# A wait for an earlier landing at every fourth gather of a graph layer's edge messages

## The chip, the cores and the metric

The kernel runs on one core of one Trainium2 chip. The metric is the device time of one execution in microseconds (us). A core has engines that run side by side, each with its own list of instructions: PE multiplies matrices, DVE and ACT do vector and scalar work, POOL issues the gathers here, and SP issues the other transfers. They meet at semaphores: an instruction may wait until a count has been reached, and everything behind it on its engine waits with it.

## The reference

There are 12500 nodes with 256 features and 212500 edges, sorted by their target node. Each edge has a source, a target and one of 8 types.

```python
h = jnp.maximum(_layernorm(x, axis=-1), 0.0)
hx = einsum('ni,rio->rno', h, weight)          # one 256 x 256 matrix for each type
agg = segment_sum(hx[edge_type, src], dst)     # sum over the edges of each target
out = x + 0.5**0.5 * agg + h_bias + 0.5**0.5 * (h @ loop_weight)
```

## The kernel before

**Sums before products.** The matrix of a type is the same for all its edges, so the kernel sums the rows of `h` first, by target and type, and multiplies afterwards. The edges are cut into 1583 tiles of 128, numbered `t`; two tiles make a unit (`PAIR` = 2). For each tile POOL gathers the 128 source rows (128 x 256 numbers, 131 KB) from DRAM into a tile `msg` (`gather`, line 832). The first 100 tiles read `x` and are normalised on the chip; the 1483 others read the table `h` that the kernel has written by then.

**The sums.** PE multiplies the gathered rows by a matrix of zeros and ones, `oh`, which DVE has made from targets and types (`edge_sums`, line 885; four matmuls for a tile, into the PSUM tile `ps`). DVE adds `ps` to a ring of sums `acc` (line 909). When all edges of a group of 128 nodes are in, PE multiplies that part of the ring by the weights (line 1070, 32 matmuls and 4 for the nodes' own rows), DVE adds the bias and `x` (lines 1083 and 1084), and SP stores four groups at a time, with loads of the next `x` and `h` rows (lines 1020 and 1089).

**Order.** Everything stands in the order in which the program issues it (a manual schedule). One loop runs over the tiles; for each `t` it issues the gathers up to `goal(t)`, then the sums of tile `t`, then bits of the other work by their costs and due times. `goal(t)` is `t + 65` (`AHEAD` = 64), less at the start.

**The gathers' own limits.** `msg` has 66 places, given out two at a time, so the gather of an even tile waits until PE has read the unit that had this place, 66 tiles earlier. It also waits on its own landing counter (eight of them, in turn), which the gather eight tiles in front of it used. Up to tile 103 a gather also waits for the last matmul of the newest unit issued so far: those gathers go "no faster than the sums". From tile 104 on nothing else holds a gather back. POOL has hardly any other work.

Of the kernel before, what the change touches and what calls it, by code (L numbers as in the profile page):

```python
# [17 lines left out]
SYNC_DEP = mybir.DependencyInfo(mybir.DependencyClass.Sync, mybir.DependencyReason.DATA)  # L18
# [36 lines left out]
QUAD = 4  # L55
LEAD = 4
PAIR = 2
# [167 lines left out]
def kernel(  # L225
# [56 lines left out]
    def place_of(t):  # L282
        u, i = divmod(t, PAIR)
        half = 0 if PAIR * u + 1 == NT else PAIR - 1 - i
        return u // P, half, u % P


    with ExitStack() as main:
# [531 lines left out]
        def gather(t):  # L820
            if t % PAIR == 0:
                both = msgs.tile([P, PAIR, D], F32, name="msg")
                for i in range(PAIR):
                    msg[t + i] = both[:, i, :]
            if t % QUAD:
                kind[t] = kind[t - 1]
            else:
                kind[t] = "h" if state["h32"] is not None and t >= state["h32"] + LATE else "x"
            table = {"h": h32, "x": x}[kind[t]]
            b, i, u = place_of(t)  # L830
            at = i * P + u
            i = nc.gpsimd.indirect_dma_start(  # L832
                out=msg[t], out_offset=None, in_=table[:, :],
                in_offset=bass.IndirectOffsetOnAxis(ap=gidx[b][:, at : at + 1], axis=0))
            if t < STARTED + STEEP * (AHEAD - STARTED) and "unit" in latest:
                tc.add_manual_dep(
                    i.ins, latest["unit"], SYNC_DEP, reason="no faster than the sums")

        def goal(t):

            return min(t + AHEAD + 1, STARTED + STEEP * (t // PAIR * PAIR))
# [50 lines left out]
            return ps  # L892

        sums = {}
        latest, made = {"pe": None}, {}

        order = RING + WIN

# [217 lines left out]
        with tc.manual_schedule():  # L1116
# [19 lines left out]
            for t in range(min(STARTED, NT)):  # L1136
                gather(t)
# [94 lines left out]
            for t in range(NT):  # L1232
                done["tile"] = t
                while gathered < min(NT, goal(t)):
                    gather(gathered)
                    gathered += 1
# [121 lines left out]
```

## Time and profile before

| | |
|---|---|
| Median of 3 runs | 2395.17 us (2394.54 to 2396.05) |
| The profiled execution: its time, its span | 2423.11 us, 2421.4 us |
| PE busy with matmuls | 1958.0 us, 81% of the span |
| DVE, POOL busy | 1328.4 us (55%), 1507.4 us (62%) |
| Granted PE clock, mean | 0.901 |
| Gathers (line 832) | 1583, from 4.9 us to 2335.6 us |
| Gathers' packets | 207.59 MB, 29.5% of 16 DMA engines' span |

How to read the profile: PE is TensorE's matmuls, PEld its weight loads, and each instruction has the line of the source that made it. A row `out<-in` tells what is written from what. In brackets behind an instruction stands how long its engine had been idle before it, and what ended the idle time; "issue" means that the engine waited for nothing that the profile shows, "remote" that the releaser could not be named. A gather on POOL is shown for as long as POOL writes its descriptors, not until its data are there; when they land is read from the packets and semaphore records of the same trace.

### The profile page before, as it was taken

Reading aid. Unit: us, or ns where it says so; the run is one execution under the profiler, and the core shown is the slowest. Engines: PE = TensorE matmul, PEld = TensorE weight load, DVE = VectorE, ACT = ScalarE, POOL = GpSimd, SP = SyncE. Lnnn points to the kernel's source line nnn. Section 1 sums busy time; section 2 is a strip of 40 time slices with the busy share of each in tenths; the row PEclk is TensorE's granted clock in tenths of the full one; section 3 lists DMA queues with packets and bytes.
Section 4 is the critical chain, followed back from the end, with each engine's and each line's share of the span. In section 5 each row is a group of like instructions: output and inputs, shape, how many; then the busy total and the mean of one; then the engine's idle time right before and its main releaser. Section 6 shows DMA issues by size and latency. Waiting matters only on the chain. (4 is left out here: it accounts for less than half of the span.)

```text
span 2421.4 us, 28275 instructions
## 1 busy us (share of the span) xinstructions
PE 1958.0 (81%) x10171; PEld 1693.8 (70%) x10171; DVE 1328.4 (55%) x3162; ACT 186.6 (8%) x363; POOL 1507.4 (62%) x1608
## 2 busy tenths in 40 slices
PE   2357888888888888888888888788888888888899
PEld 1256677777677777777777777777777777777788
DVE  5668344445655446654446654555755545655453
ACT  6653000000000000000000000000000000000000
POOL 6566666666666666666666666666666666666630
PEclk9578989898999998999988989999899899988999
DMA  7973433433333333333343333343343333343320
GB/s 235 306 227 86 125 92 114 123 91 116 115 90 116 104 112 114 92 113 116 91 123 118 87 118 114 92 122 102 105 116 89 117 117 91 114 118 88 111 69 13
DMA packets 147864, 278.81 MB, mean 115 GB/s; under 512 B 29759, under 2 KB 97064, under 8 KB 147720
## 3 DMA queue, kind: packets, MB, share of 16 engines
q0 software_dynamic: 75984, 207.59, 29.5%
q1 hardware_dynamic: 70136, 69.38, 8.9%
q8 instruction: 80, 1.31, 0.2%
q14 instruction: 64, 0.52, 0.1%
q10 hardware_dynamic: 1600, 0.01, 0.0%
HBM read 251.26 MB, written 25.60 MB: 114 GB/s over the span
## 5 line engine op out<-in xcount | busy, mean ns | idle before, releaser
L832 POOL DMA_INDIRECT msg<-h,gidx x1483 | 1410.6, 951 | 770.8 <-issue 382.3
L885 PE MATMUL ps<-oh,msg 128*128 128x176 f32 (+1 forms) x6332 | 1191.9, 314 | 289.7 <-issue 195.6
L885 PEld LDWEIGHTS ps<-oh,msg 128*128 128x128 f32 x6332 | 1088.2, 207 | 436.1 <-issue 260.6
L1070 PE MATMUL po<-w,acc 128*128 128x256 f32 x3136 | 968.6, 410 | 106.1 <-issue 86.5
L909 DVE TENSOR_TENSOR acc<-acc,ps 128x352 f32 x792 | 409.6, 517 | 779.4 <-remote 413.3
L1070 PEld LDWEIGHTS po<-w,acc 128*128 128x128 f32 x3136 | 569.4, 204 | 190.2 <-issue 138.6
L852 DVE TENSOR_TENSOR oh<-fixed,cols 128x704 f32<-128x704 f32 x397 | 349.0, 880 | 0.0
L951 DVE SCALAR_TENSOR_TENSOR acc<-types,pt 128x256 f32<-128x256 bf16 (+1 forms) x688 | 247.2, 412 | 136.8 <-PE ps L885 63.7
L934 ACT ACTIVATE self_t<-pt 128x256 f32<-128x256 f32 x98 | 37.5, 383 | 1634.0 <-DVE acc L951 899.2
L1070 PE MATMUL po<-wl,self_t 128*128 128x256 f32 x392 | 120.6, 427 | 16.0 <-issue 8.5
L832 POOL DMA_INDIRECT msg<-in_x_dram,gidx x100 | 95.0, 950 | 57.6 <-issue 33.7
L1070 PEld LDWEIGHTS po<-wl,self_t 128*128 128x128 f32 x392 | 73.6, 210 | 32.9 <-issue 18.1
L929 PE MATMUL pt<-ident,hr 128*128 128x128 f32 x196 | 42.4, 294 | 29.5 <-issue 24.7
L929 PEld LDWEIGHTS pt<-ident,hr 128*128 128x128 f32 x196 | 27.7, 158 | 39.7 <-issue 38.8
L1083 DVE TENSOR_TENSOR xr<-xr,po 128x256 f32<-128x256 f32 x98 | 40.5, 413 | 24.7 <-remote 15.4
L794 ACT ACTIVATE msg<-msg,shift,rstd 128x256 f32<-128x256 f32 x100 | 50.7, 586 | 9.5 <-DVE shift L791 5.8
L794 ACT ACTIVATE xt<-xt,shift,rstd 128x256 f32<-128x256 f32 x98 | 50.0, 587 | 8.4 <-issue 2.8
L1006 ACT ACTIVATE types<-pt 128x512 bf16<-128x512 f32 x22 | 13.1, 597 | 425.9 <-remote 207.9
L1084 DVE TENSOR_TENSOR xr<-xr,po 128x256 f32<-128x256 f32 x98 | 41.2, 421 | 3.4
L764 DVE BATCH_NORM_STATS2 stats<-xt 128x6 f32<-128x256 f32 x98 | 34.1, 413 | 16.1 <-DMA xt<-in_x_dram 13.5
L401 DVE TENSOR_SCALAR moves<-fixed 128x271 int32<-128x271 int32 (+1 forms) x90 | 40.6, 451 | 3.7 <-DVE acc L909 1.9
L403 DVE COPY_PREDICATED fixed<-moves,fixed 128x311 int32<-128x311 int32 (+14 forms) x90 | 38.0, 422 | 4.0 <-DVE moves L401 0.9
(153 smaller groups left out, 329.7 us busy)
## 6 DMA issues: line engine op xcount, KB each, us to landing
msg<-h,gidx POOLq DMA_INDIRECT x1483
xt<-in_x_dram SPq DMA_DIRECT2D x24, 512.0 KB
h<-xt SPq DMA_DIRECT2D x24, 512.0 KB
xr<-in_x_dram SPq DMA_DIRECT2D x24, 512.0 KB
hr<-h SPq DMA_DIRECT2D x24, 512.0 KB
out_dram<-xr SPq DMA_DIRECT2D x24, 512.0 KB
w<-in_L_gnn_weight_dram SPq DMA_DIRECT2D x2, 1024.0 KB
msg<-in_x_dram,gidx POOLq DMA_INDIRECT x100
```

The source lines that it names most:

```text
L401: nc.vector.tensor_single_scalar(m, packed[:, :n], 1 << (bit + k), op=ALU.bitwise_and)
L403: nc.vector.copy_predicated(packed[:, : n - (1 << k)], m[:, 1 << k :], packed[:, 1 << k : n])
L794: nc.scalar.activation(row, row, AF.Relu, bias=shift[:n, j : j + 1], scale=rstd[:n, j : j + 1])
L832: i = nc.gpsimd.indirect_dma_start(out=msg[t], out_offset=None, in_=table[:, :], in_offset=bass.IndirectOffsetOnAxis(ap=gidx[b][:, at : at ...
L852: j = nc.vector.tensor_tensor(o[:, k : k + v, :i, :], iota_f.unsqueeze(1).unsqueeze(1).to_broadcast([P, v, i, C]), of.unsqueeze(3).to_broa ...
L885: j = nc.tensor.matmul(ps[:, c, :width], m[:, c * P : (c + 1) * P], o[:, :width], start=(i == 0 and c == 0), stop=(end and c == KC - 1))
L909: i = nc.vector.tensor_tensor(a, a, ps, op=ALU.add)
L929: in_run("turns", nc.tensor.transpose(pst[:, c, :n], rows_[:n, c * P : (c + 1) * P], ident[:n, :n]), c == KC - 1)
L951: i = nc.vector.scalar_tensor_tensor(acc[:, :, r, s0 : s0 + n], of, float(r + 1), pst[:, :, :n], op0=ALU.is_equal, op1=ALU.mult)
L1070: i = nc.tensor.matmul(got["out", g][:n], lhs, rhs, start=(r == R and c == 0), stop=(r == R - 1 and c == KC - 1))
L1083: nc.vector.tensor_add(rows_[:n, k, :], rows_[:n, k, :], outs[g % 2][:n, 1, :])
L1084: nc.vector.tensor_add(rows_[:n, k, :], rows_[:n, k, :], got["out", g][:n])
```

## The change

`gather` writes down the name of each tile's gather instruction. From tile 104 on, a gather whose number is a multiple of four gets one more wait: the gather two tiles in front of it must have landed.

```diff
             if t < STARTED + STEEP * (AHEAD - STARTED) and "unit" in latest:
                 tc.add_manual_dep(
                     i.ins, latest["unit"], SYNC_DEP, reason="no faster than the sums")
+            elif t % QUAD == 0 and "unit" in latest:
+                tc.add_manual_dep(
+                    i.ins, landed[t - PAIR], SYNC_DEP, reason="one tile under way")
+            landed[t] = i.ins.name
...
-        latest, made = {"pe": None}, {}
+        latest, made, landed = {"pe": None}, {}, {}
```

`STARTED + STEEP * (AHEAD - STARTED)` is 104, `QUAD` is 4. In the lists of instructions PE, DVE, ACT and SP have the same instructions with the same waits as before. On POOL the same 1583 gathers stand in the same order. A gather whose number is a multiple of four waits for its own landing counter, for the counter of the gather two in front, and for PE; the even gathers between lose the wait for their own landing counter (which the wait before them already covers) and keep the one for PE.

## The prediction

> **What bounds the kernel now.** I read the page first, then the waits, the timeline around one stall, and a table of two stretches. In the page's costliest groups I look at the gathers and the sums:
>
> ```profile
> L832 POOL DMA_INDIRECT msg<-h,gidx x1483 | 1410.6, 951 | 770.8 <-issue 382.3
> L885 PE MATMUL ps<-oh,msg 128*128 128x176 f32 (+1 forms) x6332 | 1191.9, 314 | 289.7 <-issue 195.6
> ```
>
> One gather keeps POOL busy for 0.951 us. The waits from 300 to 2335 us say what the engines sat idle for:
>
> ```profile
> POOL msg L832 <- issue: 346.5, 1131, 0.7
> PEld ps L885 <- issue: 232.6, 347, 2.0
> POOL msg L832 <- remote: 223.7, 135, 2.7
> ...
> PE ps L885 <- issue: 173.2, 294, 1.7
> PEld po L1070 <- issue: 150.6, 240, 4.9
> POOL msg L832 <- PE ps L885: 119.1, 91, 3.1
> ```
>
> POOL's "issue" row is the ordinary gap between two gathers, 346.5 / 1131 = 0.31 us, so at full speed a gather takes 0.951 + 0.304 = 1.255 us. The tiles take 2421.4 / 1583 = 1.53 us on average. POOL is faster, and its real idle time (223.7 + 119.1 us) is waiting for PE to free a place in `msg`. No row of PE waiting for a gather is among the large ones. PE's large waits are "issue": it waits for nothing that is shown. The timeline tells when:
>
> ```profile
> 1013.53 0.95 POOL L832 DMA_INDIRECT msg<-h,gidx  x1 [0.30 <-issue]
> ...
> 1014.10 0.38 PE L1070 MATMUL po<-w,acc 128*128 128x256 f32 x1
> 1015.50 0.19 PEld L1070 LDWEIGHTS po<-w,acc 128*128 128x128 f32 x1 [1.45 <-issue]
> 1015.50 0.48 PE L1070 MATMUL po<-w,acc 128*128 128x256 f32 x1 [1.03 <-issue]
> 1015.61 0.19 PEld L885 LDWEIGHTS ps<-oh,msg 128*128 128x128 f32 x1
> 1016.23 0.76 PE L885 MATMUL ps<-oh,msg 128*128 128x176 f32 x4 [0.25 <-issue]
> ...
> 1016.54 0.95 POOL L832 DMA_INDIRECT msg<-h,gidx  x1 [2.06 <-remote]
> ```
>
> PE starves at 1014.1 while gathers run. POOL ends its gather at 1014.48, finds no free place and pauses; PE then moves again (1015.50, full speed from 1016.23), frees a place, and POOL starts its next burst at 1016.54. Over the whole trace I counted 142 such stalls between 250 and 2335 us (gaps over 0.6 us between starts of weight loads and matmuls, taken together when under 2.5 us apart), one about every 15 us. They begin 8 to 12 us after a burst of gathers began, PE gets a pair of instructions every 0.71 us or a small multiple of it while they last, and 133 of the 142 have a POOL pause in them, with PE moving freely again typically 1.05 or 2.1 us after the pause began. Without gathers there are none:
>
> ```profile
> 2200.00:2275.00 75.00, 61.51 (x333) 52.57 (x332) 35.23 (x76) 1.75 (x4) 47.57 (x52) 0.91 0.37 106
> 2340.00:2415.00 75.00, 75.00 (x429) 68.58 (x428) 35.33 (x74) 1.29 (x3) 0.00 (x0) 1.00 0.03 10
> ```
>
> The first figures are PE's busy time and matmuls, the fifth pair POOL's. With 52 gathers beside it PE does 333 matmuls, without any 429. So I read the kernel as a cycle: about 9 gathers in a burst, PE starves, POOL runs out of places and pauses, PE is fed. The end is PE's, and the pace is POOL's burst plus the pause that PE needs.
>
> The Trainium skill speaks against that reading: "SBUF — State Buffer", section "Who interferes with whom", says that a DMA never contends with a compute engine and that PE waits on no one. By that rule the gathers are beside the path and the sum would be 0. The two stretches above do not bear it out for PE's stream of instructions, whatever the memory's ports do, so it stays as a rival with a small chance.
>
> **The change, part by part.** *Removed:* the own-counter wait of every other even gather. It was always satisfied (eight gathers, over 10 us, back): 0 us.
>
> *Added:* 370 waits (t = 104, 108, ... 1580). Behind each stand on POOL only the later gathers, and PE needs their rows about 64 tiles x 1.53 = 98 us later, so PE never waits for the rows themselves. What the wait costs is POOL's time. From the packet records a gather lands 2.43 us after its start in the middle, and the middle half lies between 2.40 and 2.47. The gather two behind would start 2 x 1.255 = 2.51 us after it, so in ordinary flow the wait is nearly over. But a wait that ends late has to reach POOL and start the gather. The trace shows no such wait on a landing; from PE's semaphore to a gather's start, where POOL sat idle, I find 0.1 to 0.3 us, and I take 0.30, because here the wait needs an instruction of its own before the gather. Then t starts at 2.43 + 0.30 = 2.73 after t - 2 instead of 2.51, some 0.2 us late. Going through all 370 with their recorded landings and starts:
> - Term A: 313 whose predecessor flew under 2.7 us. 230 would be late, 0.21 us each in the middle, 49 us together. (The rest lie behind a pause of POOL and cost nothing.)
> - Term B: 57 whose predecessor flew 2.7 to 6.3 us, because SP's four-group loads and stores were under way. 49 would be late, 1.5 us each, 72 us together.
>
> *How much of it reaches the end.* If the pace is the burst plus the pause, a longer burst makes the cycle longer, except that PE creeps on meanwhile: two instructions in 0.71 us, 2.8 per us against 20342 / 2421 = 8.4 on average, one third. So of term A two thirds pass: 49 x 2/3 = 33 us; its bounds are 0 (the short pause feeds PE as well as a long one) and 49. In term B a wait of 1.5 us is as long as the pauses of POOL that set PE free (1.3 to 2.4 us), so most of it should stand in place of such a pause; bounds 0 and 72 x 2/3 = 48, and I take 10. Below nothing: a pause placed better than now could even gain, see the rivals.
>
> Sum: 33 + 10 = 43 us on the profiled 2423.1, so 2466 us; against the median of runs, 43 x 2395.17 / 2423.11 = 42.5, so 2438 us. SP's loads may land sooner with fewer gathers in front of them; PE shows no wait on them, so 0.
>
> **The rivals.** *No change (chance 0.14).* Pauses feed PE by their total length, wherever they lie. A straight-line fit over the stretches between stalls gives PE 7.2 instructions per us in a burst and 10 more for each us of pause; with the number of gathers fixed, the time then does not depend on how the pauses are spread. That gives 2395. For it: the fit does not need a dead time at the start of a pause. Against it: in the timeline PE creeps on for about 1 us into a pause. That the new wait does nothing at all is unlikely, with 279 of 370 ending late by the records; the skill's rule of untroubled compute would give 2395 as well.
>
> *Faster (chance 0.28).* The short, regular pauses feed PE before it starves. The new pauses, 49 + 72 = 121 us, would replace 121 / 1.8 = 67 of the some 200 long ones (2.1 us less the ordinary 0.3), and each long one that is gone saves PE the 1 us in which it still creeps: up to 70 us; a third of it, 23 us, gives 2372. It decides if the 0.5 us pause at every fourth gather is long enough for PE to get instructions. For it: no gather data move between the landing of t - 2 and those of t - 1 for part of the time, and slow spells during SP's loads get long pauses for sure. Against it: t - 1 is still in flight then, and in 79 long pauses inside a stall PE's rate rose only from about 0.65 us after the gather's end on.
>
> *Slower by much (inside the forecast's chance).* All of A and B passes on undiminished: 121 us, 2395 + 120 = 2515. That would need PE to get nothing out of the long waits of term B, against the pauses seen, so I keep 2485 as the end of the range.
>
> **How the numbers follow.** Slower, as forecast: 0.58. No change: 0.14. Faster: 0.28. The prediction is the forecast's 2438 us. A measurement of this kernel can tell about 0.2%, 5 us. The forecast's own range is 2405 to 2485; to leave out no more than 2 in 10 the range must take in no change and most of the faster case: 2372 to 2485.
>
> **What the profile after would show.** POOL's gaps before every fourth gather grow from 0.30 to about 0.5 us, released by a landing of `msg`; POOL's row for waits on PE or "remote" shrinks, from 343 us to perhaps 260. PE's "issue" waits stay or grow. If instead PE's "issue" rows of 173 and 233 us shrink clearly and PE's stalls grow rarer, the short pauses do feed PE and the forecast is wrong in its step on how much reaches the end. If no gather shows a landing as its releaser, the wait's size (terms A and B) is wrong. If PE shows waits on the gathers, the 98 us of lead was an error.

## The result, and the profile after

The changed kernel takes 2507.65 us (median of 4 runs, 2505.44 to 2515.64) against 2395.26 us on the same chip: a ratio of 1.046, 95% interval [1.044, 1.048]. That is 112 us slower, 70 more than forecast and 23 above the upper end of the range. The profiled execution took 2505.44 us, its span is 2503.7 us, the mean granted clock 0.918.

The costliest groups of the changed kernel (line 889 is line 885 of before):

```profile
L832 POOL DMA_INDIRECT msg<-h,gidx x1483 | 1405.8, 948 | 921.1 <-issue 673.1
L889 PE MATMUL ps<-oh,msg 128*128 128x176 f32 (+1 forms) x6332 | 1216.3, 320 | 481.0 <-DMA msg<-h,gidx 378.1
L889 PEld LDWEIGHTS ps<-oh,msg 128*128 128x128 f32 x6332 | 1013.4, 203 | 789.1 <-DMA msg<-h,gidx 638.8
```

A gather costs POOL about what it cost before (948 ns against 951). POOL's idle time has grown from 771 to 921 us. What ends most of the idle time ahead of PE's sums is now the landing of a gather. The waits from 300 to 2440 us say it in full:

```profile
POOL msg L832 <- issue: 637.5, 1194, 6.1
PEld ps L889 <- DMA msg<-h,gidx: 628.3, 732, 4.7
...
PE ps L889 <- DMA msg<-h,gidx: 371.1, 404, 4.4
```

PE's issue rows, 232.6 and 173.2 us before, are down to these:

```profile
PEld ps L889 <- issue: 11.8, 22, 2.8
...
PE ps L889 <- issue: 6.9, 16, 2.4
```

So PE hardly ever sits idle any more without a wait that is shown: it waits for rows. POOL's timeline shows why (start, duration, and in brackets the idle time before):

```profile
1016.94 0.94 POOL L832 DMA_INDIRECT msg<-h,gidx  x1 [1.36 <-issue]
1018.19 1.15 POOL L832 DMA_INDIRECT msg<-h,gidx  x1 [0.30 <-issue]
1019.64 0.95 POOL L832 DMA_INDIRECT msg<-h,gidx  x1 [0.30 <-issue]
1020.89 0.95 POOL L832 DMA_INDIRECT msg<-h,gidx  x1 [0.30 <-issue]
1023.16 0.94 POOL L832 DMA_INDIRECT msg<-h,gidx  x1 [1.32 <-issue]
```

The pause before each fourth gather is 1.34 us in the middle. By the packet records the waiting gather starts 1.12 us after the landing it waits for, and 96 of 100 start between 1.08 and 1.61 us after it. The wait stands in a semaphore instruction of its own in front of the gather. That instruction's record ends 0.40 us after the landing in the middle, and the gather starts 0.72 us behind it. The releaser column rarely names the landing: it says "issue" for 227 of the 370 waiting gathers and a landing for 40.

**Where the 1.34 us lead.** Without the slow flights four gathers now take POOL 4 x 1.254 + 1.03 = 6.05 us, 1.51 us a tile; with them the trace has (2477.3 - 158.1) / 1478 = 1.57 us a tile, from tile 104 to the last. PE took 1.47 us a tile before (tiles 300 to 1500; the 1.53 of the prediction is the mean of the whole span, slow start included). POOL has become the slower of the two, and the lead (from the landing of a tile to its first matmul) runs out:

| tile | 104 | 200 | 300 | 800 | 1500 |
|---|---|---|---|---|---|
| lead before, us | 88.0 | 85.1 | 85.6 | 87.0 | 84.6 |
| lead after, us | 87.0 | 29.4 | 0.4 | 0.6 | 0.4 |

**The account in POOL's time.** POOL's gaps beyond the ordinary 0.305 us, from tile 104 on, sum to 318.8 us before and 469.3 us after, of which 454 stand before the fourth gathers. POOL's old pauses, in which it waited for a place in `msg`, are gone with the lead. From tile 104 to the last gather the time grows by 144 us, from 2175.1 to 2319.2 (the gaps' 150 less some 5 us, as a gather took 3 ns less). The part behind the last gather shrinks from 85.8 to 26.4 us, because PE has nothing left to catch up on, and the part ahead of tile 104 by 2.4. That is +144.1 - 59.4 - 2.4 = +82.3 us, the difference of the two spans. The profiled execution of before was 28 us longer than the median of its runs, which with the 2 us on the other side makes up the rest of the 112.

### The profile page after: what moved, and what is told of

It reads as the page before. It is cut to its first block, busy times and chain, and to the rows that moved or that the text cites. A ratio compares the mean times of both kernels' runs of the same rounds, so it can differ in the third digit from the quotient of the medians.

```text
span 2503.7 us, 27941 instructions
## 1 busy us (share of the span) xinstructions
PE 1977.3 (79%) x10171; PEld 1607.3 (64%) x10171; DVE 1347.1 (54%) x3162; ACT 186.7 (7%) x363; POOL 1502.4 (60%) x1608
## 3 DMA queue, kind: packets, MB, share of 16 engines
q8 instruction: 80, 1.31, 0.2%
## 5 line engine op out<-in xcount | busy, mean ns | idle before, releaser
L889 PE MATMUL ps<-oh,msg 128*128 128x176 f32 (+1 forms) x6332 | 1216.3, 320 | 481.0 <-DMA msg<-h,gidx 378.1
L889 PEld LDWEIGHTS ps<-oh,msg 128*128 128x128 f32 x6332 | 1013.4, 203 | 789.1 <-DMA msg<-h,gidx 638.8
L1074 PE MATMUL po<-w,acc 128*128 128x256 f32 x3136 | 903.9, 394 | 11.0 <-DVE acc L913 6.7
L1074 PEld LDWEIGHTS po<-w,acc 128*128 128x128 f32 x3136 | 546.9, 197 | 48.2 <-issue 7.7
L1074 PE MATMUL po<-wl,self_t 128*128 128x256 f32 x392 | 139.6, 491 | 12.2 <-issue 9.4
L1074 PEld LDWEIGHTS po<-wl,self_t 128*128 128x128 f32 x392 | 89.0, 250 | 25.8 <-issue 11.9
L994 DVE TENSOR_TENSOR of<-pt,line 22x512 bf16<-22x512 f32 x22 | 15.0, 682 | 50.1 <-PE pt L987 43.5
```

Source lines behind the costliest of these rows:

```text
L889: j = nc.tensor.matmul(ps[:, c, :width], m[:, c * P : (c + 1) * P], o[:, :width], start=(i == 0 and c == 0), stop=(end and c == KC - 1))
L1074: i = nc.tensor.matmul(got["out", g][:n], lhs, rhs, start=(r == R and c == 0), stop=(r == R - 1 and c == KC - 1))
```

## The experiments

The theory at this point: the waiting gather starts 1.1 us after a landing, that makes POOL the bound, and PE's starving hides a part of the price. The rivals: the wait as such costs time, or PE loses a share of its time with each pause. The runs fell on different chips, so ratios to the kernel before on the same chip are compared. All diffs are against the changed kernel, but for e8's, which is against the kernel before.

| run | wait | us | kernel before there | ratio, interval |
|---|---|---|---|---|
| e1 | every 4th, on t - 4 | 2403.11 | 2396.54 | 1.003 [1.001, 1.004] |
| e2 | every 4th, on t - 3 | 2428.72 | 2396.54 | 1.014 [1.012, 1.015] |
| e3 | every 8th, on t - 2 | 2451.89 | 2396.54 | 1.023 [1.022, 1.025] |
| e4 | every 4th, odd, on t - 2 | 2452.28 | 2396.54 | 1.024 [1.022, 1.025] |
| e5 | every 10th, odd, on t - 1 | 2499.12 | 2427.55 | 1.030 [1.025, 1.036] |
| e6 | every 8th, odd, on t - 1 | 2422.81 | 2427.55 | 0.998 [0.996, 0.999] |
| e7 | every 2nd, on t - 2 | 2937.91 | 2427.55 | 1.211 [1.208, 1.214] |
| e8 | none, half of the gathers | 1814.04 | 2427.55 | 0.748 [0.746, 0.749] |
| e9 | every 6th, on t - 2 | 2352.66 | 2028.34 | 1.159 [1.157, 1.161] |
| e10 | every 7th, on t - 2 | 2266.44 | 2028.34 | 1.118 [1.116, 1.120] |
| e11 | 8 and 10 in turn, odd, on t - 1 | 2362.87 | 2028.34 | 1.165 [1.162, 1.168] |
| e12 | every 5th, on t - 2 | 2359.29 | 2028.34 | 1.164 [1.162, 1.166] |
| f1 | the kernel before | 2426.87 | 2425.01 | 1.000 [0.999, 1.002] |
| f2 | the change | 2514.32 | 2425.01 | 1.036 [1.034, 1.039] |
| f3 | e3 again | 2476.13 | 2425.01 | 1.020 [1.017, 1.023] |
| f4 | e8 again | 1814.44 | 2425.01 | 0.748 [0.746, 0.750] |
| g1 | e9 again | 2356.82 | 2029.45 | 1.161 [1.159, 1.163] |
| g2 | e11 again | 2366.94 | 2029.45 | 1.167 [1.165, 1.168] |

**Is it the wait, or that it ends late?** In e1 the landing waited for is that of four tiles back, in e2 of three.

```diff
-                    i.ins, landed[t - PAIR], SYNC_DEP, reason="one tile under way")
+                    i.ins, landed[t - 4], SYNC_DEP, reason="one tile under way")
```

> The same 370 waits, but on the gather four in front instead of two. Theory A (a gather behind such a wait starts 1.10 us after the landing, as in the trace after, and POOL's longer pace of 6.04 us for four gathers, 1.51 each, then binds): four in front lands 2.42 us after its start, and 2.42 + 1.10 = 3.52 lies well before the 4 x 1.254 = 5.02 at which the gather starts anyway. Only flights over 3.9 us, under one in ten, would be late. Time 2390 to 2410 us, POOL's gaps 0.30 us again, PE with issue stalls as before. Rival B (the price is in the wait itself, late or not: one more thing for POOL to do): about 2500 us. The recorded prediction's theory (only lateness costs, 0.2 us of it) also gives 2395.

> The same 370 waits, on the gather three in front. Theory A: 2.42 + 1.10 = 3.52 us against a start at 3 x 1.254 = 3.76 us, so still 0.24 us in time; late only behind flights over 2.66 us, some 45 waits of 1 to 2 us, of which POOL has 340 us to spare: 2395 to 2420 us. Rival C (the 1.1 us are not counted from the landing; POOL loses about 1 us wherever its list is held until a landing that comes after the newest gather but one began): POOL's gap at every fourth gather near 1.3 us and 2480 us or more. This run is the sharp one, since A leaves it only 0.24 us.

In e1 the same 370 waits cost 0.3%: POOL's gaps at these gathers are 0.30 us again in the middle, and the lead is kept to the end. By the landings plus 1.12 us, 18 of the 370 hold POOL, for 25 us together. The instruction is nearly free, its lateness is the price. In e2 it is 34 of the 370, for 57 us together, and it costs 1.4%. (Gaps over 0.4 us alone don't tell: 102 of the same gathers have one in before, where they wait for a place in `msg`.)

**Fewer waits.** e3 waits at every eighth gather.

```diff
-            elif t % QUAD == 0 and "unit" in latest:
+            elif t % 8 == 0 and "unit" in latest:
```

> The wait on the gather two in front, at every eighth gather only (185 waits). Theory A: eight gathers take 8 x 1.254 + 1.03 = 11.06 us, 1.38 a tile, less than the 1.53 that PE took before, so POOL is no longer the bound and PE does not wait for rows. What then sets the time is PE's feeding: if pauses of 1.3 us every 11 us keep PE from starving (in the trace after, with one every 6 us, PE's issue waits fell from 406 to 19 us on the sums' lines), the time falls below before, down to 158 + 1479 x 1.38 + 90 = 2290 us; if only the sum of the pauses counts, 2395. The recorded prediction's way of counting (two thirds of the lateness reaches the end): 2395 + 185 x 1.03 x 2/3 = 2522 us.

The start is 1.12 us after the landing again and the pause 1.36 us. POOL is not the bound: the lead stays at 74 to 88 us at the tiles of the table. But the kernel is not faster than before, it is 2.3% slower, and PE starves as it did in before (waits from 300 to 2200 us):

```profile
PEld ps L889 <- issue: 219.0, 356, 2.0
...
PE ps L889 <- issue: 149.3, 257, 2.1
...
PEld ps L889 <- DMA msg<-h,gidx: 5.1, 9, 1.1
```

Stalls (counted as in the prediction, from 300 us to the last gather) are fewer and longer: 99 with 6.05 us in the middle, 647 us in all, against 139 with 3.7 and 534 in before. The time in which PE was granted half its clock grew from 354 to 498 us. So a wait has two prices: POOL's time where POOL is the bound, and where it is not, stalls of PE that a short pause doesn't end. The second is read from the stalls of this run and the next; no run isolates it.

**What the 1.10 us are made of.** In e4 the odd gather t % 4 = 1 waits on t - 2, and the gather itself carries that wait (odd gathers don't wait for a place; the gather ahead also waits for t - 7, long landed, which covers the odd one's own counter).

```diff
-            elif t % QUAD == 0 and "unit" in latest:
+            elif t % QUAD < 2 and "unit" in latest:
                 tc.add_manual_dep(
-                    i.ins, landed[t - PAIR], SYNC_DEP, reason="one tile under way")
+                    i.ins, landed[t - (PAIR if t % QUAD else 7)], SYNC_DEP,
+                    reason="one tile under way")
```

> The wait on the gather two in front stands at the odd gathers t = 4k + 1, which do not wait for PE. The gather before each also waits for the one seven in front of it (long landed), which makes the odd gather's other wait needless, so the landing is the only wait that it carries and no instruction of its own is needed for it. Theory A1 (the 1.10 us come from a wait that stands in an instruction of its own in front of the gather, so that the gather is made ready only afterwards): the gather starts 0.1 to 0.3 us after the landing, POOL's gap there is 0.3 to 0.5 us, four gathers take about 5.1 us, and the time is 2380 to 2440. Theory A2 (any wait on a landing wakes POOL 1.1 us later): gap 1.3 us, 6.04 us for four, about 2500 us.

The timeline of POOL in e4:

```profile
1004.63 0.95 POOL L832 DMA_INDIRECT msg<-h,gidx  x1 [0.30 <-issue]
1006.36 0.94 POOL L832 DMA_INDIRECT msg<-h,gidx  x1 [0.79 <-DMA msg<-h,gidx]
```

The gather starts 0.60 us (0.58 to 0.63) after the landing and the profile now names the landing. So 0.5 of the 1.1 us comes from the wait standing in an instruction of its own; the other 0.6 is between the landing and a gather that waits on it by itself. The lead is kept, but the pauses of 0.81 us feed PE even less: 83 stalls of 6.4 us, 712 us together, and 2.4% more time.

**Long pauses.** e5 and e6 wait for the gather just in front, whose flight can't be over: every tenth and every eighth gather, the wait carried by the gather. This is e6's edit; e5 has 10 in place of 8.

```diff
-            elif t % QUAD == 0 and "unit" in latest:
+            elif t % 8 < 2 and "unit" in latest:
                 tc.add_manual_dep(
-                    i.ins, landed[t - PAIR], SYNC_DEP, reason="one tile under way")
+                    i.ins, landed[t - (1 if t % 8 else 7)], SYNC_DEP,
+                    reason="one tile under way")
```

> From tile 104 on the gathers t = 10k + 1 wait until the gather right in front has landed; the gather before each also waits for the one seven in front (long landed), so that the odd gather carries the landing as its only wait. The gap is then 2.42 + 0.60 - 0.95 = 2.07 us at every tenth gather, and ten gathers take 10 x 1.254 + 1.77 = 14.3 us, 1.43 a tile. Theory S (PE starves while POOL issues without a long pause; pauses of 1.9 us or more inside a stall ended it in 40 of 41 cases or better, those of 0.8 us in 10 of 115): each pause feeds PE, about in time, so 158 + 1479 x 1.43 + 86 = 2360 us, up to 2400 if ten gathers are a little too many. Rival (every forced pause is lost time beside those that PE needs anyway, as the 2452 us with a pause of 1.33 us at every eighth would also allow): 148 pauses, 2430 to 2450.

> The same at t = 8k + 1: a gap of 2.07 us at every eighth gather, where the run with the wait two back at every eighth had 1.33 us and took 2452 us. Eight gathers take 10.03 + 1.77 = 11.8 us, 1.475 a tile. Theory S: a pause that is longer by 0.7 us feeds PE where the shorter one did not, PE's issue waits (about 480 us on the sums' and products' lines there) fall by half or more, and the time comes down although POOL loses 130 us more: 158 + 1479 x 1.475 + 86 = 2425 us. Rival (lost POOL time is lost): above 2452, up to 2560.

Both pause for 2.07 us. With ten gathers between (e5) PE starves for 605 us, 3.0% slower. With eight (e6) it hardly starves, and POOL is the bound:

```profile
PEld ps L890 <- DMA msg<-h,gidx: 426.3, 457, 5.6
...
PE ps L890 <- DMA msg<-h,gidx: 258.5, 214, 5.2
...
PEld ps L890 <- issue: 42.7, 69, 2.0
...
PE ps L890 <- issue: 29.3, 58, 1.5
```

e6 loses more POOL time than e3 (380 us against 345) and is 2.6 points faster against its kernel before. POOL's time alone doesn't order these kernels; whether a pause ends a stall does. Counting pauses that begin inside a stall, and how many see it end by 1 us after the pause:

| pause, us | stalls ended | from |
|---|---|---|
| 0.6 to 1.0 | 10 of 115 | e4 |
| 1.2 to 1.5 | 26 of 45; 23 of 57 | before; e3 |
| 1.9 to 2.3 | 41 of 41; 18 of 19; 77 of 81 | before; e3; e5 |

In before a pause ends because PE has freed a place, so its rows can't tell which came first, and a longer pause is also given a longer count. With only the added waits, and 3.07 us counted from each pause's start, the order stays: 28 of 108 in e4 (0.81 us), 16 of 44 in e3 (1.36), 59 of 62 in e5 (2.07).

**More waits, and half of the gathers.** e7 waits at every even gather. e8 has no added wait; from tile 104 on it leaves out the odd tiles' gathers and sums the even tile's rows twice.

```diff
             table = {"h": h32, "x": x}[kind[t]]
+            if t >= 104 and t % PAIR:
+                msg[t] = msg[t - 1]
+                return
```

> The wait on the gather two in front at every second gather (740 waits). Theory A (start 1.10 us after the landing, POOL's pace is the time): two gathers take 2.42 + 1.10 = 3.52 us, 1.76 a tile; 158 + 1479 x 1.76 + 26 = 2787 us, and about 100 us more for the long flights: 2790 to 2900. The recorded prediction's price of 0.2 us a wait would give 148 us in all, 2540. If POOL's time were hidden anyway: 2500 as with half as many waits.

> The kernel before, with the odd tiles' gathers left out from tile 104 on: PE multiplies the even tile's rows twice, so the sums are of the wrong rows, and all work but half of the gathers is there. Theory S (the gathers starve PE of instructions): POOL has 1.25 us of work in two tiles, pauses all the time, and PE's issue waits fall from 480 us to under 60; the time falls to about 1.25 us a tile, as in the stretch without gathers, 158 + 1479 x 1.25 + 20 = 2030 us. Rival (PE's issue waits come from its own list, not from the gathers): 2350 to 2395 us.

e7's 740 waits take it to 2938 us, 1% above the range that POOL's pace gave, and PE waits for rows. e8 takes 1814 us, less than expected, with the same 10171 matmuls; its page:

```profile
PE 1682.2 (93%) x10171; PEld 1555.0 (86%) x10171; DVE 1325.2 (73%) x3162; ACT 186.6 (10%) x363; POOL 803.9 (44%) x869
...
PEclk9557999999999999999999999999999999999999
```

In the waits from 300 to 2200 us (e8 ends at 1811) one issue row for `ps` is left, against 392.8 us in before:

```profile
PEld ps L888 <- issue: 5.2, 13, 0.4
```

PE has the same instructions and gets them without starving once half of the gathers are gone. That "issue" means starving for instructions is a reading: the rows say only that nothing shown was waited for. A late transfer of PE's list is not borne out. The packets hold 80 instruction transfers of 16 KB, one for about 254 of PE's 20342 instructions; they took 1.0 us each in the middle in before, in e8 and in e9 alike, and the stalls of before begin anywhere between two of them. Whether it is POOL's work on a gather or the gather's data that holds PE back was not separated.

**Other spacings, on another kind of chip.** e9, e10 and e12 wait at every sixth, seventh and fifth gather; e11 puts e6's long pauses after eight and ten gathers in turn.

> The change at every sixth gather (t%6 == 0 waits for the gather two tiles in front of it). Both theories: the waiting gather starts 1.10 us after that landing, the pause before it is 1.35 us, and POOL needs (6 x 1.254 + 1.03) / 6 = 1.43 us for a tile, with about 0.04 us for the long flights 1.47, so POOL is not the bound. Theory S (a pause of 1.35 us often ends no stall of PE's issue, so that what counts is how often one comes while PE starves): six gathers between pauses lie between the four that keep PE fed and the eight that don't; the time lies between every eighth's 1.023 and a fed PE's 0.985 of the kernel before, about 1.01. Rival P (POOL's lost time is all that counts): 1.00.

> The change at every seventh gather (t%7 == 0, two tiles back). POOL needs (7 x 1.254 + 1.03) / 7 = 1.40 us for a tile and isn't the bound. Theory S: nearly as starved as with every eighth, 1.015 to 1.025 of the kernel before. Rival P: POOL loses less than with every sixth, 0.98 to 1.00.

> Long pauses (one tile back, the wait carried by the gather itself, 2.07 us as with every eighth and every tenth before) after eight and ten gathers in turn, nine in the mean. POOL needs 1.254 + 1.77/9 = 1.45 us for a tile, with the long flights 1.49, less than the 1.51 of every eighth that was the bound there. Theory S: the long pause ends PE's stall every time, so the time lies between every eighth's 0.998 and what the pace of 1.49 would give, 0.985. Rival: the bursts of ten are already too long, as in the kernel with every tenth (1.030), and the time is 1.01 or more.

> The change at every fifth gather (t%5 == 0, two tiles back). POOL needs (5 x 1.254 + 1.03) / 5 = 1.46 us for a tile, with the long flights 1.50, where every fourth needs 1.55: if POOL's pace is what set the time of the change, the time falls to about 2400 us at the first chip's scale, 1.00 of the kernel before, and the lead of the gathers over PE is used up much later or never. Rival (the waits cost PE by themselves, whatever POOL's pace): between 1.02 and 1.046, in line with every fourth and every eighth.

The chip of these four runs the kernel before in 2028 us, in 15% less time than the others, so the ratios missed everywhere. The cause is in the waits of e9 (300 to 2200 us):

```profile
PEld ps L889 <- DMA msg<-h,gidx: 520.8, 652, 4.9
...
PE ps L889 <- DMA msg<-h,gidx: 291.4, 329, 4.7
...
PEld ps L889 <- issue: 1.7, 4, 0.4
```

PE doesn't starve on this chip in any of the four kernels (at most 4 us in that row), not even after ten gathers in a row (e11). A kernel bound by POOL shows little starving anyway, but e6, bound by POOL on a chip of the first kind, has 42.7 us there and e11 1.2. All four run at POOL's pace with a lead of 0.5 to 0.6 us in the middle from tile 300 on, and the price is one of POOL alone: over 2028.34 us, (2266.44 - 2028.34) / 212 waits = 1.12 us a wait in e10, 331 / 296 = 1.12 in e12, 324 / 246 = 1.32 in e9, 334.5 / 164 = 2.04 in e11. POOL's gaps at these waits, beyond the ordinary 0.305 us, come to nearly the same sums: 327 us in e9, 240 in e10, 330 in e12, 337 in e11. (In e10 and e12 half of the waits are at odd gathers, which carry them: their pause is 0.8 us as in e4, that of the even ones 1.3, so the same edit shows both kinds of wait.) The kernel before itself fits POOL's unbroken pace there: 142 us up to tile 104, 1479 x 1.254, and 26 behind the last gather make 2023 us. No profile of it was taken on such a chip, so that this is its bound is inferred.

**The two kernels again, profiled on one chip.** f1 to f4 are before, the change, e3 and e8.

> The kernel before, unchanged, for its profile on the chip of this call. If that chip runs it in about 2028 us: gathers follow each other every 1.254 us with nearly no pauses from tile 104 (at about 142 us) to the last, 142 + 1479 x 1.254 + 26 = 2023, and PE shows under 30 us of waits on issue in ps rows. If it takes 2395 to 2430 us: the profile of before again, PE's issue waits 400 us or so and POOL's pauses 320 us. A third outcome speaks against both: 2028 us with PE's issue waits still there.

> The change, unchanged, on the chip of this call. If the change's price is POOL's pace alone, the time is the same on every chip: 370 waits of 1.05 us and the long flights, 454 us on 142 + 1853 + 26, so 2475 to 2510 us; that is 1.22 to 1.24 of the kernel before where that takes 2028 us, and 1.03 to 1.05 where it takes 2395 to 2430. Rival (the waits cost PE a share of its time, the same on every chip): 1.046 there too, 2122 us on a chip with 2028.

> The change at every eighth gather, as before. On a chip where PE doesn't starve, POOL's sum is 142 + 1853 + 185 x 1.17 (as much for a wait as with every seventh gather there) + 26 = 2237 us, 1.10 of 2028 and 215 us below what it took where PE starves (2452). On a chip where PE starves: 1.02 again.

> Half of the gathers left out from tile 104 on, the rows of the even tiles used twice, as before. PE was 93% busy in it, so that it is PE's own pace and doesn't depend on the chip: 1814 us, 0.894 of 2028 or 0.75 of 2395 to 2430. If PE is faster on a chip without starving even here, 1750 us or less.

They ran on a chip where PE starves: f1 shows 237.1 and 167.2 us of issue waits in the `ps` rows (300 to 2200 us), much as before did (224.9 and 167.9). There the kernel before is 30 us slower than on the chip of the result (2425 against 2395) and the change only 7 (2514 against 2508, 4 us above the expected range): so between these two chips what is bound by POOL varied less than what is bound by PE's starving. f3 repeats e3 in its ratio (1.020 against 1.023), and f4 repeats e8 to 0.4 us.

**Two of the spacings again.**

> The change at every sixth gather once more. It took 2353 us on the chip where the kernel before takes 2028, all of it POOL's sum. On a chip where the kernel before takes 2395 to 2430 us: if its pauses of 1.35 us keep PE fed, 2350 to 2380 us, 0.97 to 0.98 of the kernel before, and PE waits for rows; if they don't (theory S), 2430 to 2470 us, 1.00 to 1.02, with PE's issue waits of some 200 to 400 us in ps rows and the lead of the gathers kept longer.

> The long pauses after eight and ten gathers in turn once more. It took 2363 us on the chip where the kernel before takes 2028. On a chip where the kernel before takes 2395 to 2430 us: theory S gives 2365 to 2430 us, 0.975 to 1.00, as the long pause ends a stall nearly every time; the rival (bursts of ten are too long) 2450 us or more, 1.01 or more, with PE's issue waits above 200 us in ps rows.

These fell on another chip with a fast kernel before (2029 us) and only repeat e9 and e11. Whether a pause at every sixth gather would end the starving on the first kind of chip stays open, as does what sets the two kinds apart; and the change itself wasn't run on the fast kind. By the 454 us of its own pauses, or by e9's 1.32 us for each of its 370 waits, it would cost some 454 to 490 us on 2028, a ratio of 1.22 to 1.24 (an estimate). No kernel here beats both clearly: e6 is 0.2% under the kernel before where PE starves, and by e11's 2.04 us a wait its 185 waits would cost some 380 us on the other kind (an estimate again).

## Why the prediction was wrong

**Right: what bounds the kernel before.** The cycle of a burst, a starving PE and a pause that feeds it holds on this kind of chip: leaving out half of the gathers takes PE's issue waits away (e8), only pauses near 2 us end a stall reliably (the table above), and with such pauses a burst of ten is too long where eight is not (e5, e6). The Trainium skill's rule that was set against it ("SBUF — State Buffer", "Who interferes with whom": a DMA never contends with a compute engine) stands there among rules on the memory's ports. Taken as a rule on all of PE's time it isn't borne out: by it e8 would leave PE's issue waits as they were, and in the sums' rows they fell from 392.8 to 5.2 us, with the time from 2427 to 1814. On the chips of e9 to e12, g1 and g2 the traces are in line with it (4.0 us at most). What the prediction couldn't see from one profile is that the starving comes with the chip.

**Right: the wait that was removed is worth nothing, as far as is known.** No run takes it away alone, and none shows a gain from it.

**Right, but by luck: the direction.** Slower was forecast for a longer burst beside a starving PE; it came from POOL's pace.

**Wrong, and the step that failed: the price from release to start, and with it terms A and B.** I took 0.30 us, the upper end of bounds of 0.1 to 0.3 that came from releases by PE's semaphore. A landing takes 1.12 us when the wait is an instruction of its own, and 0.60 when the gather carries it. The margin in ordinary flow was 2.51 - 2.43 = 0.08 us, so the lateness is the price itself less 0.08: 0.2 us at 0.30, but 1.0 us at 1.12. Term A was to be 230 late gathers with 49 us; it is 333 gathers, all late, with 345 us. Term B was 72 us; it is 37 gathers with 110. Together 454 us instead of 121. The price alone makes most of the step: counted over the starts of before as in the prediction, 1.12 us gives 296 late gathers and 357 us. In the run POOL's old pauses, behind which a wait cost nothing, are gone too. The bounds didn't hold for this wait: those rows were of another kind of release, and nothing in the trace bounded this one from above.

**Wrong as a consequence: the lead.** "PE never waits for the rows themselves" rested on a lead of 98 us, about what the trace shows (85 to 88). But a lead only covers a wait while the pace behind it is the faster one, and the 1.53 us a tile that POOL was set against were 1.47 behind the slow start. With 0.30 us POOL would have needed 1.254 + 0.22 / 4 = 1.31 us a tile in ordinary flow and kept the lead; with 1.12 it needs 1.51 before the slow flights, and the lead is used up within 200 tiles. The prediction named PE's waits on gathers as what would show this error, and they are the largest rows of PE now.

**Wrong: how much reaches the end.** Two thirds of A and 10 us of B were to pass on, because PE creeps on during a burst. In the new regime POOL sets the pace, and everything that POOL loses passes on; in return the old pauses (319 us) and the tail (59 us) are saved. That is why 454 us of new pauses cost 82 between the two spans and not 454. "Slower by much" put 2515 us, near the result, but by another mechanism (PE getting nothing out of the pauses), while the traces show PE fed: its issue waits all but vanish.

**The faster rival** was right that new pauses feed PE, and wrong on their size: at 0.8 us they hardly do (e4), at 1.35 a third to two in five do (e3), and by the time they come often enough POOL is the bound.

**The signs.** POOL's gap of about 0.5 us: 1.34. PE's issue waits stay or grow: they shrink. POOL's waits on PE for a place are gone with the lead; the 82.9 us that its row on PE's sums still has lie mostly at the waiting gathers. The sign "no gather shows a landing as its releaser" was badly chosen: the column names a landing for 40 of the 370 (64 us) and "issue" for 227 (337 us), although nearly each ends a fixed time after a landing. The packet records show it, the releaser column shows little of it.

## What to carry to other kernels

Before a wait is added to a producer with a long lead, compare its new pace, price of the late wait included, with the consumer's: a lead hides a delay that comes once, and none that comes at every fourth step. A price taken from another kind of release (an engine's semaphore) is no bound for a landing; where no row shows it, work out the price at which the bound changes hands (here 4 x (1.47 - 1.254) + 0.08 = 0.94 us with no slow flights, about 0.65 us with the 110 us that they cost in the run; estimates) and ask if it can be excluded. And where an engine starves beside transfers, a pause has to be long enough, not only frequent.

## What was not expected of the hardware

- A gather that POOL holds for a landing starts 1.12 us after it when the wait is an instruction of its own in front, 0.60 us when the gather carries the wait (e4).
- On some chips PE stalls with nothing shown to wait for while gathers run: 2395 to 2428 us for the kernel before on those, 2028 to 2029 on two others. The cause is open. On the first kind a pause of POOL of 1.9 us and more ended a stall in 136 of 141 cases, one under 1.0 us in 10 of 115.
- Long stalls go with a lower PE clock: half clock for 354 us in before (stalls of 3.7 us in the middle), 498 in e3 (6.05), 239 in the changed kernel (1.6), from 300 to 2340 us in each.
